# A two-layer convolution block on one core: a third buffer for the residual rows, and small products moved ahead of the big ones

## The chip, the cores and the metric

One core of a Trainium2 chip (trn2) runs the whole program in one launch. The metric is the device time in microseconds of that core, as the median of several runs. Engines are named as the profile names them: PE (matrix products), PEld (loading of the products' fixed operand), DVE (vector), ACT (scalar, with its own DMA queue), POOL (GpSimd) and SP (issues most DMAs and does nothing else).

## The reference

Input x is four images (B = 4) of 64 channels and 256 x 256 pixels, in float32. Two layers follow each other, and each adds its result to its input.

```python
# layer 0: x = x + L0(groupnorm(x)), groups of two channels
h = gelu(conv3x3(x, c1_w) + c1_b)
xa, k = split(c1x1(h, c2_w) + c2_b)            # 64 and 64 channels
xs = gelu(conv_3x1(conv_1x3(xa)))              # one filter per channel
weights = softmax(mean(xs) @ gate_w.T)         # two of three experts are kept
out = xs + sum_i mask_i * c1x1(c1x1(k, w2_i) * c1x1(xs, w1_i), w3_i)   # ranks 2, 4, 8
L0 = c1x1(out, proj_w) + proj_b
# layer 1: x = x + L1(groupnorm(x))
w1, w2 = quantize(w1), quantize(w2)            # 8 bit grid, one scale per tensor
h = relu(batchnorm(conv3x3(x, w1) + b1))       # statistics over all four images
h = batchnorm(conv3x3(h, w2) + b2)
L1 = relu(h + x)
```

The mean over all pixels in the gate of layer 0, and the batch norm of layer 1, make it necessary that a whole image (or all four) has passed one stage before the next begins.

## The kernel before, in words

The two partition halves hold two blocks of rows of the 64 channels. A chunk is 128 partitions by 2048 numbers (1 MB), and an image has 16 of them (`NCH`).

**Layer 0, the slots.** After the statistics of image 0, the program runs 64 slots, one per chunk of the four images, with one slot per chunk `u`. A slot is two steps of a plan: `at_slot(u, pos, ...)` files a call, positions below 6 in the first step and the others in the second. The plan is sorted by step and position and played in that order, and every engine keeps to it. So an instruction that waits holds up all that comes later on its own engine or queue. In a slot PE does:

- at 1 and 1.3 the products (1, 2) and (3, 4) of a 3x3 convolution in a transformed domain (`front_conv`, PSUM tag "c", two buffers, the tile `ps_c`),
- at 2 and 4 the taps of the depthwise filter for an earlier chunk (`front_taps_a`, `front_taps_b`; tile `ps_a`, a single buffer),
- at 5 the products (0, 5), which are added on top of what DVE's `butterfly_c` (4.05) left in the same PSUM tile,
- at 7 and 9 the other half of the taps,
- at 8, between those two, the low-rank branches: `front_k` in even slots (tile `ps_k`), `front_q` in odd ones (tile `ps_q`), both in the single buffer of PSUM tag "p".

The single `ps_a` buffer comes free when ACT (`front_taps_i`, L699) and DVE (`front_taps_h`, L706 to L717) have turned it into the tile `t`. A slot's inner products leave through `front_h(u, True)` on ACT (L658), after DVE's `butterfly_d`; that frees the buffer into which the next slot's products (1, 2) go.

**Layer 0, the outputs.** Once the gate of image b is known, from slot 16(b+1)+4 on, each slot also makes one chunk of outputs of image b: `out_load` (L835) reads the chunk of x into a tile `y` of pool tag "o" with two buffers, `out_open` forms the product, `out_add` (L880, DVE) adds, and `out_store` (L893) writes the tile to `y_d` in DRAM. The statistics of image b+1 or b+2 are read and made in the same slots (`stats_load`, L410; `stats_group` on DVE, `stats_piece` on ACT). The last five chunks of image 2 and all of image 3 are done later, beside layer 1 (`plan_out_late`).

```python
def out_load(b, k):
    ys[b, k] = chunk_out(f"y_{b}_{k}", "o", 2)
    nc.sync.dma_start(flat(ys[b, k]), io["xp"][b, k])
```

**Layer 1.** `plan_conv1` starts in the last slots of layer 0. Each chunk's results h (`conv1_out`, L318 on DVE) are written into a tile and stored to `h1_d`. Odd chunks use `chunk_x`, a place that layer 0 has left, even ones and the first three the single buffer "h1" of the pool `conv1`. After all four images come the second convolution (`conv2`), which keeps to PE, and the end, which reads and writes whole chunks by DMA.

`weights1` makes the quantized weights of layer 1 on DVE during image 0; `stats_end` turns an image's statistics into mean and scale.

Of the kernel before, what the change touches and what calls it, by code (L numbers as in the profile page):

```python
# [9 lines left out]
F32 = mybir.dt.float32  # L10
# [9 lines left out]
P = 128  # L20
# [21 lines left out]
def conv_preact_kernel(ctx: ExitStack, tc: tile.TileContext, io, col128, colset, col64):  # L42
# [81 lines left out]
    nc.vector.memset(eps, GN_EPS)  # L124
    eps_bn = const.tile([P, 1], F32, name="eps_bn")
    nc.vector.memset(eps_bn, BN_EPS)
    zeros = const.tile([P, PW], F32, name="zeros")
# [11 lines left out]
    end, ends, edge_bias = column("end", 2), column("ends", 2), column("edge_bias", 2)  # L139
    outer = lconst.tile([P, 2, W], F32, name="outer")  # L140
    u_raw = lconst.tile([P, 6, 3, C], F32, name="u_raw")
# [32 lines left out]
    def weights():  # L174
# [24 lines left out]
        for i in range(2):  # L199
            o = outer[:, i, :]  # L200
            nc.vector.tensor_scalar(o, zeros[:, 0:W], sh_bias, None, ALU.add)
            nc.vector.tensor_tensor(o[:, 0 : W : W - 1], o[:, 0 : W : W - 1], end, ALU.subtract)
            nc.vector.tensor_scalar(o, o, c128("sv")[:, 2 * i : 2 * i + 1], None, ALU.mult)

# [40 lines left out]
    def weights1(name):  # L245

        scale = w_scale[name]
        w = mset[0][:, colset[name][0] : colset[name][1]]
        nc.vector.tensor_scalar(scale, scale, 1.0 / QMAX, None, ALU.mult)
        inv = stat.tile([P, 1], F32, tag="s3", name=f"inv_{name}")  # L250
        nc.vector.reciprocal(inv, scale)
        yield
        nc.vector.tensor_scalar(w, w, inv, ROUND, ALU.mult, ALU.add)
        nc.vector.tensor_scalar(w, w, ROUND, None, ALU.subtract)
        nc.vector.tensor_scalar(w, w, QMAX, -QMAX, ALU.min, ALU.max)
        yield
        g = w.rearrange("p (k o) -> p k o", k=3)
        first, second = g[:, :, 0:P], g[:, :, P : 2 * P]
        nc.vector.tensor_copy(wq[name][:, 0], first)
        nc.vector.tensor_tensor(wq[name][:, 1], first, second, ALU.add)  # L260
        nc.vector.tensor_scalar(wq[name][:, 2], second, -1.0, None, ALU.mult)
# [439 lines left out]
    def front_taps_h(u, sub):  # L701
# [19 lines left out]
        for at_n, i, row in ((0, 0, 0), (NOCT - 1, 1, 2 * GP - 1)):  # L721
            if n == at_n:
                rows = slice(i * C, i * C + C)
                nc.vector.tensor_tensor(t[rows, row, :], t[rows, row, :], outer[rows, i, :], ALU.subtract)

# [33 lines left out]

    def front_q(b, j):  # L760

        ps = ps_q[b, j] = bank("p", f"ps_q_{b}_{j}").rearrange("p s a b -> p s (a b)")
        for s in range(2):
            for i in range(4):
                x = xss[b, 4 * j + i][:, s]
# [67 lines left out]
    def out_load(b, k):  # L833
        ys[b, k] = chunk_out(f"y_{b}_{k}", "o", 2)
        nc.sync.dma_start(flat(ys[b, k]), io["xp"][b, k])  # L835
# [132 lines left out]
    def conv1_out(b, k, g):  # L968
        if g == 0:
            if k % 2 and (b > 0 or k > 2):  # L970
                h_out[b, k] = flat(chunk_x(f"h1_{b}_{k}"))[:, 0 : CPAIR * W].rearrange("p (a b) -> p a b", b=W)
# [111 lines left out]
    def plan_front():  # L1083
# [4 lines left out]
        for u in range(SLOTS):  # L1088
# [34 lines left out]
            if 0 <= u - 1 <= last:  # L1123
# [30 lines left out]
        for i, name in enumerate(("w1", "w2")):  # L1154
            chain = weights1(name)
            for n in range(3):
                at_slot(7 + 3 * i + n, 7.3, next, chain, None)

    def plan_stats(b):
# [4 lines left out]
        for k in range(NCH):  # L1164
# [13 lines left out]
        places = (e, 8.3), (e + 1, 1.25), (e + 1, 1.36), (e + 2, 1.25), (e + 2, 1.36), (e + 2, 4.45), (e + 2, 8.3), (e + 3, 1.25), (e + 3, 1.36)  # L1178
        chain = stats_end(b)
# [26 lines left out]
    def plan_out_late(b, ns, steps, order, end):  # L1206

        for n, step in zip(ns, steps):
# [22 lines left out]
    def plan_conv1(b):  # L1231
# [4 lines left out]
        for k in range(NCH):  # L1236
# [59 lines left out]
    def bn_affine(mv, gamma, beta, out, name):  # L1296

        ms = stat.tile([P, 2], F32, tag="ms", name=f"ms_{name}")
        for _ in combine(mv, B, c128("avg2"), eps_bn, ms, name):
            pass  # L1300
# [334 lines left out]
```

## Time and profile before

| what | us |
|---|---|
| median of 3 runs | 2964.82 (2963.71 to 2973.92) |
| the profiled execution, its time | 2959.65 |
| the profiled execution, its span on the core | 2957.8 |
| PE busy in the span | 2345.4 (79%) |
| DVE busy | 2448.4 (83%) |
| ACT busy | 2007.1 (68%) |
| POOL busy | 1676.8 (57%) |
| DMA moved, mean | 309 GB/s |

In the profiled execution, layer 0's slots run from about 57 to 1252, the first convolution of layer 1 from about 1270 to 1965, the second to about 2524, and the end to 2958. Shares over the whole span mix these stages, so the stages are read one at a time. A slot begins where PE's products (1, 2) begin, which is where a slot's length is read from.

### The profile page before, as it was taken

To read this page: it belongs to the slowest core of one execution; us is meant where nothing else is said; L and a number is where in the kernel's file an instruction comes from. 1 tells how busy PE (TensorE), PEld (TensorE's weight loads), DVE (VectorE), ACT (ScalarE), POOL (GpSimd) and SP (SyncE) were. 2 spreads that over 40 slices of the span, in tenths; PEclk is the share of its full clock that TensorE was granted. 3 is DMA by queue.
4 is the path that set the end of the run, shared out by engine and by line. 5 is a ranking of instruction groups with operands and counts; after the bars stand their busy time and mean duration, and the time that the engine had idled before them with its cause. 6 is when DMAs were issued, how large, how long until landed. Compare 5 with 4: busy or idle time off the path is not lost.

```text
span 2957.8 us, 52737 instructions
## 1 busy us (share of the span) xinstructions
PE 2345.4 (79%) x21576; PEld 1502.1 (51%) x21576; DVE 2448.4 (83%) x2811; ACT 2007.1 (68%) x2183; POOL 1676.8 (57%) x1252
## 2 busy tenths in 40 slices
PE   2888899999999999979999999989999999000000
PEld 1444445444445555546666667867788888000000
DVE  6688678888888988869999999979999898976664
ACT  4777888787776665567676667978888887432221
POOL 6988888787778888733545546735555555000000
PEclk9999999999999999999999999999999999555555
DMA  8665579999999999859999997747777764999999
GB/s 352 233 239 209 199 269 369 354 351 350 355 349 320 320 319 327 290 203 320 343 367 361 332 360 272 270 176 274 258 267 264 270 219 156 375 412 423 420 424 409
DMA packets 135715, 915.35 MB, mean 309 GB/s; under 512 B 14960, under 2 KB 15728, under 8 KB 40880
## 3 DMA queue, kind: packets, MB, share of 16 engines
q1 hardware_dynamic: 107824, 777.74, 71.1%
q10 hardware_dynamic: 27648, 134.23, 11.3%
q8 instruction: 170, 2.79, 0.4%
q14 instruction: 73, 0.60, 0.1%
HBM read 573.74 MB, written 338.17 MB: 308 GB/s over the span
## 4 chain that ended last, share of the span: by engine, by line
PE 50%; DMA 29%; DVE 13%; ACT 3%; POOL 2%; issue 2%; SPq 0%; ACTq 0%; DVEq 0%; POOLq 0%
PE ps_h L296 18%; PE ps_c L513 9%; DMA y<-in_xp 7%; PE ps_a L513 7%; PE ps_h2m L296 6%; DMA y_end<-y_d 5%; DMA y_d<-y 4%; DMA out<-h 4%; DMA h<-h_d 4%; PE ps_o L513 4%; DMA yn<-y_d 3%; PE ps_hm L296 3%; DVE t L714 2%; DVE t L717 2%; PE ps_k L744 1%
## 5 line engine op out<-in xcount | busy, mean ns | idle before, releaser
L296 PE MATMUL ps_h<-diff,w_q 128*128 128x512 f32 x3072 | 755.2, 400 | 12.4 <-DVE h L318 11.9
L296 PEld LDWEIGHTS ps_h<-diff,w_q 128*128 128x128 f32 x3072 | 577.0, 189 | 190.6 <-issue 20.4
L513 PE MATMUL ps_c<-v,us 64*64 64x256 f32 x9216 | 534.0, 380 | 28.6 <-DVE ps_c L644 25.4
L343 POOL TENSOR_TENSOR d<-yn 128x1024 f32<-128x1024 f32 x128 | 348.9, 2745 | 299.3 <-DMA yn<-y_d 164.8
L513 PEld LDWEIGHTS ps_c<-v,us 64*64 64x64 f32 x9216 | 360.7, 134 | 174.4 <-issue 17.6
L343 POOL TENSOR_TENSOR d<-h 128x1024 f32<-128x1024 f32 x126 | 307.1, 2459 | 206.4 <-DVE diff L351 143.6
L513 PE MATMUL ps_a<-h,av 64*64 64x512 f32 x4080 | 386.5, 492 | 47.3 <-DVE t L717 40.1
L318 DVE SCALAR_TENSOR_TENSOR h<-ps_h,scale_w,m 128x1024 f32<-128x1024 f32 x256 | 323.1, 1279 | 78.7 <-PE ps_h L296 56.3
L561 POOL TENSOR_TENSOR x<-x 128x512 f32<-128x512 f32 x256 | 328.8, 1284 | 12.7
L1497 ACT ACTIVATE h<-h,shift,gn 128x2048 f32<-128x2048 f32 (+1 forms) x65 | 134.3, 2067 | 276.0 <-DVE h L1496 273.8
L513 PEld LDWEIGHTS ps_a<-h,av 64*64 64x64 f32 x4080 | 153.7, 133 | 322.2 <-issue 212.8
L382 ACT ACTIVATE junk<-h,less_h 128x2048 bf16<-128x2048 f32 (+3 forms) x134 | 256.2, 1912 | 13.6 <-DVE h L318 13.5
L1496 DVE SCALAR_TENSOR_TENSOR h<-h,inverse,y_end 128x2048 f32<-128x2048 f32 (+1 forms) x65 | 150.5, 2317 | 122.0 <-DMA y_end<-y_d 122.0
L699 ACT ACTIVATE t<-ps_a,tap_bias,m 128x1016 f32<-128x1016 f32 x128 | 153.3, 1197 | 117.0 <-PE ps_a L513 91.4
L880 DVE SCALAR_TENSOR_TENSOR y<-ps_o,ob,y 128x1024 f32<-128x1024 f32 x128 | 164.0, 1281 | 50.9 <-PE ps_o L513 26.6
L730 ACT ACTIVATE xs<-t 128x1024 f32<-128x1024 f32 x128 | 134.8, 1053 | 103.8 <-DVE t L717 90.2
L353 DVE SCALAR_TENSOR_TENSOR diff<-d,gn,diff 128x1024 fp32r<-128x1024 f32 x128 | 202.0, 1608 | 0.9 <-ACT diff L346 0.5
L296 PE MATMUL ps_h2m<-odd,w_q 128*128 128x512 f32 x768 | 193.5, 401 | 5.9 <-ACT odd L359 3.8
L296 PE MATMUL ps_hm<-odd,w_q 128*128 128x512 f32 x768 | 194.0, 402 | 2.8 <-DVE t L717 1.3
L346 ACT ACTIVATE diff<-d 128x1024 fp32r<-128x1024 f32 x128 | 135.3, 1057 | 81.1 <-POOL d L343 79.5
L553 POOL TENSOR_TENSOR x<-x,x 128x512 f32<-128x512 f32 x128 | 160.5, 1275 | 34.2 <-ACT x L547 34.2
L717 DVE SCALAR_TENSOR_TENSOR t<-ps_a,m,t 128x1020 f32<-128x1020 f32 x128 | 163.9, 1280 | 4.6
(256 smaller groups left out, 4235.2 us busy)
## 6 DMA issues: line engine op xcount, KB each, us to landing
x<-in_xc SPq DMA_DIRECT2D x64, 1280.0 KB
h<-h_d SPq DMA_DIRECT2D x64, 1152.0 KB
yn<-y_d SPq DMA_DIRECT2D x60, 1152.0 KB
xs_in<-in_xp SPq DMA_DIRECT2D x64, 1024.0 KB
xs_d<-xs ACTq DMA_DIRECT2D x128, 512.0 KB
xs_in<-xs_d SPq DMA_DIRECT2D x64, 1024.0 KB
y<-in_xp SPq DMA_DIRECT2D x64, 1024.0 KB
y_d<-y SPq DMA_DIRECT2D x64, 1024.0 KB
```

The lines of the kernel that those rows point to most:

```text
L296: nc.tensor.matmul(ps, wq[w][:, kind, kx, :], t[:, rows, kx : kx + W], start=(j == 0), stop=(j == len(terms) - 1))
L318: nc.vector.scalar_tensor_tensor(h.rearrange("p (e k) w -> p e (k w)", e=2), ps.rearrange("p e k w -> p e (k w)"), w_scale[w], m.unsqueeze ...
L343: engine.tensor_tensor(raw.rearrange("p (g r) w -> p g r w", g=2), *pair, ALU.subtract)
L353: nc.vector.scalar_tensor_tensor(lower, raw, scale, upper.bitcast(F32), ALU.mult, ALU.subtract)
L382: nc.scalar.activation(junk[rows, 0:n], flat(h), AF.Square, bias=less[name][rows], accum_out=total)
L513: last[:] = [nc.tensor.matmul(ps[o, at_out[0] : at_out[1], :], w[i], rhs[i], **flags)]
L553: nc.gpsimd.tensor_tensor(x4[:, j - 1], x_rows(u, j + 2), x4[:, j - 1], ALU.subtract)
L561: nc.gpsimd.tensor_tensor(x[:, r : r + 2], x[:, r + 2 : r + 4], x[:, r : r + 2], ALU.subtract)
L699: nc.scalar.activation(t[:, :, inside], ps[:, :, inside], AF.Identity, bias=tap_bias, scale=sh[:, 1:2])
L717: nc.vector.scalar_tensor_tensor(t[:, :, 0 : W - 1], ps[:, :, 1:W], sh[:, 2:3], t[:, :, 0 : W - 1], ALU.mult, ALU.add)
L880: nc.vector.scalar_tensor_tensor(y, ps.rearrange("p x s w -> p x (s w)"), out_bias[b], y, ALU.add, ALU.add)
L1496: nc.vector.scalar_tensor_tensor(at_h, at_h, inverse[:, b : b + 1], y[:, a:e, :], ALU.mult, ALU.add)
```

## The change

It has these parts:

1. A third place for the outputs' tile `y`: chunks with k % 3 == 2 take a tile "third" in the pool `front`, for images 0 and 1 and the first 11 chunks of image 2. Space for it comes from `outer` (two rows of W numbers become one, half the partitions each) and from `eps_bn`, which had the value of `eps`.
2. In slots before 20 (`alone`), `front_k` and the first three of four units of `front_q` move from position 8 to 4.5, ahead of the products (0, 5). The fourth unit of `front_q` stays at 8.
3. `weights1` is cut into four steps rather than three, in other slots. `stats_group` of image 1 moves behind `butterfly_d` (6.125), and the first step of `stats_end` for image 1 from 8.3 to 6.126.
4. The results of chunk 1 of image 0 in layer 1 go to `chunk_x`. The differences of that chunk are made behind the taps of the last slots.
5. `out_store` in `plan_out_late` goes one step later. In SP's order, image 3's stores of `y` from chunk 7 on now stand behind a load `yn`.

```diff
-    outer = lconst.tile([P, 2, W], F32, name="outer")
+    outer = lconst.tile([P, W], F32, name="outer")
...
         nc.vector.reciprocal(inv, scale)
-        yield
         nc.vector.tensor_scalar(w, w, inv, ROUND, ALU.mult, ALU.add)
+        yield
         nc.vector.tensor_scalar(w, w, ROUND, None, ALU.subtract)
+        yield
         nc.vector.tensor_scalar(w, w, QMAX, -QMAX, ALU.min, ALU.max)
...
-    def front_q(b, j):
-        ps = ps_q[b, j] = bank("p", f"ps_q_{b}_{j}").rearrange("p s a b -> p s (a b)")
+    def front_q(b, j, units=range(4)):
+        if 0 in units:
+            ps_q[b, j] = bank("p", f"ps_q_{b}_{j}").rearrange("p s a b -> p s (a b)")
+        ps = ps_q[b, j]
         for s in range(2):
-            for i in range(4):
+            for i in units:
...
     def out_load(b, k):
-        ys[b, k] = chunk_out(f"y_{b}_{k}", "o", 2)
+        if k % 3 == 2 and (b < B - 2 or b == B - 2 and k < 11):
+            ys[b, k] = front_pool.tile([P, CPAIR, W], F32, tag="third", name=f"y_{b}_{k}")
+        else:
+            ys[b, k] = chunk_out(f"y_{b}_{k}", "o", 2)
...
-            if k % 2 and (b > 0 or k > 2):
+            if k % 2:
                 h_out[b, k] = flat(chunk_x(f"h1_{b}_{k}"))...
...
+            alone = u < NCH + 4
             if u % 2 == 0 and 0 <= j < UNITS // 2:
-                at_slot(u, 8, front_k, *divmod(j, NOCT // 4))
+                at_slot(u, 4.5 if alone else 8, front_k, *divmod(j, NOCT // 4))
             if u % 2 and 0 <= j < UNITS // 2:
-                at_slot(u, 8, front_q, *divmod(j, NOCT // 4))
+                if alone:
+                    at_slot(u, 4.5, front_q, *divmod(j, NOCT // 4), range(3))
+                at_slot(u, 8, front_q, *divmod(j, NOCT // 4), range(3 if alone else 0, 4))
...
-            for n in range(3):
-                at_slot(7 + 3 * i + n, 7.3, next, chain, None)
+            for u in ((5, 6, 7, 8), (9, 10, 11, 14))[i]:
+                at_slot(u, 7.3, next, chain, None)
...
-                at_slot(int(s), 4.1 if s - int(s) < 0.5 else 7.25, stats_group, b, *group)
+                early = 6.125 if int(s) < NCH else 4.1
+                at_slot(int(s), early if s - int(s) < 0.5 else 7.25, stats_group, b, *group)
...
-        places = (e, 8.3), ...
+        places = (e, 6.126 if b == 1 else 8.3), ...
...
             if n % 2:
-                at(step + 1, 13.3, out_store, b, n // 2)
+                at(step + 2, 13.3, out_store, b, n // 2)
...
+            behind = b == 0 and k == 1
-            at(*late(up0, 13.12), conv1_upper, b, k, 0)
-            at(*late(up1, 13.14), conv1_upper, b, k, 1)
+            at(*late(up0, 13.36 if behind else 13.12), conv1_upper, b, k, 0)
+            at(*late(up1, 13.37 if behind else 13.14), conv1_upper, b, k, 1)
-            at(*((t, 1.3) if first else late(low0, 13.22)), conv1_lower, b, k, 0)
+            at(*((t, 1.3) if first else late(low0, 13.45 if behind else 13.22)), conv1_lower, b, k, 0)
```

More of the change, by code (lines that the diff above doesn't have):

```diff
@@ L124, in conv_preact_kernel @@
     nc.vector.memset(eps, GN_EPS)
-    eps_bn = const.tile([P, 1], F32, name="eps_bn")
-    nc.vector.memset(eps_bn, BN_EPS)
+    assert BN_EPS == GN_EPS
     zeros = const.tile([P, PW], F32, name="zeros")
@@ L199, in weights @@
         for i in range(2):
[L200 to L203, printed above, removed]
+            rows = slice(i * C, i * C + C)
+            o = outer[rows]
+            nc.vector.tensor_scalar(o, zeros[rows, 0:W], sh_bias[rows], None, ALU.add)
+            nc.vector.tensor_tensor(o[:, 0 : W : W - 1], o[:, 0 : W : W - 1], end[rows], ALU.subtract)
+            nc.vector.tensor_scalar(o, o, c128("sv")[rows, 2 * i : 2 * i + 1], None, ALU.mult)
         nc.vector.memset(wk, 0.0)
@@ L251, in weights1 @@
         nc.vector.reciprocal(inv, scale)
+        nc.vector.tensor_scalar(w, w, inv, ROUND, ALU.mult, ALU.add)
         yield
-        nc.vector.tensor_scalar(w, w, inv, ROUND, ALU.mult, ALU.add)
         nc.vector.tensor_scalar(w, w, ROUND, None, ALU.subtract)
+        yield
         nc.vector.tensor_scalar(w, w, QMAX, -QMAX, ALU.min, ALU.max)
@@ L723, in front_taps_h @@
                 rows = slice(i * C, i * C + C)
-                nc.vector.tensor_tensor(t[rows, row, :], t[rows, row, :], outer[rows, i, :], ALU.subtract)
+                nc.vector.tensor_tensor(t[rows, row, :], t[rows, row, :], outer[rows], ALU.subtract)
     def front_xs(u, sub):
@@ L1175, in plan_stats @@
                 s = slots[k] + group[2] // 2 * per / 2
-                at_slot(int(s), 4.1 if s - int(s) < 0.5 else 7.25, stats_group, b, *group)
+                early = 6.125 if int(s) < NCH else 4.1
+                at_slot(int(s), early if s - int(s) < 0.5 else 7.25, stats_group, b, *group)
         e = NCH * b - 4
-        places = (e, 8.3), (e + 1, 1.25), (e + 1, 1.36), (e + 2, 1.25), (e + 2, 1.36), (e + 2, 4.45), (e + 2, 8.3), (e + 3, 1.25), (e + 3, 1.36)
+        places = (e, 6.126 if b == 1 else 8.3), (e + 1, 1.25), (e + 1, 1.36), (e + 2, 1.25), (e + 2, 1.36), (e + 2, 4.45), (e + 2, 8.3), (e + 3, 1.25), (e + 3, 1.36)
         chain = stats_end(b)
@@ L1298, in bn_affine @@
         ms = stat.tile([P, 2], F32, tag="ms", name=f"ms_{name}")
-        for _ in combine(mv, B, c128("avg2"), eps_bn, ms, name):
+        for _ in combine(mv, B, c128("avg2"), eps, ms, name):
             pass
```

## The prediction, made before the changed kernel ran

> **What bounds the kernel now.** I read first the busy time by stretches, because shares over the whole span mix unlike stages. I asked for three runs of slots: 23 to 25, 26 to 43 and 45 to 62.
>
> ```profile
> core 0: us, PE busy (x) PEld busy (x) DVE busy (x) ACT busy (x) POOL busy (x), PEclk, DMA share, GB/s
> 455.89:511.92 56.03, 55.89 (x805) 28.75 (x800) 50.34 (x64) 45.55 (x65) 45.94 (x43) 1.00 0.99 375
> 511.92:875.53 363.61, 340.23 (x4764) 173.59 (x4760) 300.76 (x392) 283.49 (x398) 282.31 (x282) 1.00 0.96 352
> 894.14:1233.24 339.10, 338.39 (x4764) 175.47 (x4760) 301.68 (x389) 207.21 (x256) 282.34 (x282) 1.00 0.93 321
> ```
>
> A slot is 56.03/3 = 18.68 us in the first stretch, with PE always busy, 363.61/18 = 20.20 us in the second, with 23.4 us of PE idle, and 339.10/18 = 18.84 us in the third, where no statistics are loaded. So slots 26 to 43 are not PE's. Next, for slots 26 to 43, the waits of PE (total us, times, longest), those of SP's queue, and the chain of work in order of time (start, us).
>
> ```profile
> PE ps_a L513 <- DVE t L717: 16.3, 15, 1.9
> ```
>
> ```profile
> SPq L835 <- DMA y_d<-y: 75.9, 18, 7.7
> ```
>
> ```profile
> 508.50 14.60 DMA y_d<-y
> ...
> 523.18 20.57 DMA y<-in_xp
> ...
> 549.11 14.77 DMA y_d<-y
> ```
>
> Every load of a `y` tile (L835, 18 of 18) waited for the store of the tile two chunks back. A store of 14.60 us, a load of 20.57 us, and DVE's two additions with the taps between them (543.83 to 549.09, 5.3 us) make 40.5 us for two chunks, which is the 20.2 us of a slot. DVE's addition waits for the load, and the taps `t` queue behind it, so PE waits for `t`.
>
> In image 0 I read PE's instructions in order of time, over one slot that began at 164.24, and PE's waits from 100 to 420 (second fence).
>
> ```profile
> 173.41 2.82 PE L513 MATMUL ps_c<-v,us 64*64 64x256 f32 x48 [0.77 <-DVE ps_c L644]
> 176.95 2.38 PE L513 MATMUL ps_a<-h,av 64*64 64x512 f32 x24 [0.72 <-DVE t L717]
> 179.26 1.95 PE L744 MATMUL ps_k<-h,wk 64*32 64x512 f32 x32
> ```
>
> ```profile
> PE ps_a L513 <- DVE t L717: 18.9, 20, 1.9
> PE ps_c L513 <- DVE ps_c L644: 13.9, 18, 1.1
> ```
>
> Products (0, 5) wait for the butterfly, then the taps wait for `t`, and only then comes `ps_k`, which needs neither.
>
> Where layer 1 begins, PE stands still once for long (its waits from 1250 to 1345, the chain, and two stretches with the columns as above):
>
> ```profile
> PE ps_h L296 <- DVE h L318: 8.6, 1, 8.6
> ```
>
> ```profile
> 1318.68 11.37 DMA h_d<-h
> ```
>
> ```profile
> 1319.00:1331.52 12.52, 3.95 (x16) 2.56 (x15) 1.35 (x3) 7.06 (x7) 5.62 (x3) 0.77 1.02 369
> 1331.52:1339.40 7.88, 7.88 (x26) 6.23 (x26) 7.84 (x8) 6.59 (x7) 2.96 (x2) 0.72 1.02 195
> ```
>
> DVE cannot write chunk 2's h until chunk 1's has left the single place "h1". The granted clock falls to 0.77 and 0.72 around it.
>
> **The third place for y.** It adds no instruction. A load then waits for the store three chunks back, which began more than a slot before the load's turn and takes 14.6 us, so the wait at L835 goes. What is late next is the DMA engines. A slot with outputs and statistics moves, from the KB of the issues: x 1280, statistics 1024, xs stored 2 x 512, xs read 1024, y read 1024, y stored 1024, ranks written 256 and read 256. That is 6912 KB or 7.08 MB, and 7.08/20.2 is 350 GB/s, at a DMA share of 0.96. If only the idle 4% is won, 352/0.96 = 367 GB/s, or 19.3 us a slot. The first stretch carried 375 GB/s at 0.99: 18.9 us. PE's floor is 18.63. I take 19.05, between the two, a gain of 18 x 1.15 = 21 us. The Trainium skill speaks against this ("DMA: Bandwidth & Descriptors", "Where 436 GB/s comes from"): HBM transfers are bound near 358 GB/s a core. By that rule a slot needs 7.08/358 = 19.8 us and the gain is 18 x 0.4 = 8 us. This trace moved 375 over three such slots, and 420 GB/s in the end's slices, so I follow the row, and keep 8 as the low end. The high end is PE's floor, 18 x 1.57 = 28. The order on SP's queue is the same in these slots. The load is only issued earlier, so x and xs behind it are no longer held.
>
> **k and q ahead of (0, 5), 18 slots (2 to 19).** A slot is now 17.57 us on average (92.79 to 216.76 has seven in 123.97, so 17.7; two neighbours make 17.38 + 17.76). The moved products (1.95 us, or some 1.4 for three units) cover the 0.77 before (0, 5), and push (0, 5) late enough that `t` is ready: 0.72 to 1.13. These are 1.5 to 1.9 us. Against that, in even slots the wait for the tick after the taps, 0.2 us, is bare. PE alone would come to about 16.1. What is late next: from the end of the taps at 172.6, ACT's `t` (1.2), DVE's `t` (2.85), `butterfly_d` (1.4), and then, in ACT's order, a statistics piece ahead of `h`, end at 180.4, which is 7.8 us that the move does not shorten. The next slot's products (1, 2) need that `h`'s PSUM place. The slot's start to the end of the taps is 8.4 us (164.24 to 172.6), so 8.4 + 7.8 = 16.2 is the floor on this ring, and ACT's `t` for the other half now queues behind both `h`. I put the slot at 16.8 rather than 16.2, as these waits seldom fit exactly: 0.8 x 18 = 14 us, from 5 to 23 (1.3 x 18). POOL needs 15.5 us a slot (twelve at about 1.28), so it does not bind. The skill speaks against the split of q: "TensorEngine Tiling (Array Packing)", "Key Properties", says that a change of tiling mode drains the array. Cutting `ps_q` in two adds two changes in nine slots. In the trace `ps_k` (64*32) between products of 64*64 runs in 1.95 with no idle named before or after it, and by start times `ps_q` begins 2.3 us after the taps' 2.38 began. So I price a change at zero to 0.2 us, at most 9 x 0.4 = 4 us, which the low end holds.
>
> **Weights, statistics, outer.** Of the slots, that from 216.76 lasts 19.11: DVE's three operations on `mset` (1.39, 1.51, 1.54 us) stand ahead of `t`, which then was late by 1.24. Spread, with one of about 1.4 us a slot, this costs nothing while DVE has its 3 us of slack. If that cover is gone, it is 1.5 us in each of some eight slots. I count +1.5 here, and as much from the second weight, from `first`'s statistics behind the butterfly and from POOL's sums ahead of its differences (`ps_m_x` waited 0.82): together 3 us, 0 to 5. `outer` removes nothing on the path (it is before slot 0), nor does `eps_bn`.
>
> **Layer 1's start.** With chunk 1 in `chunk_x`, chunk 2's h needs the store of chunk 0, issued at 1303.9, and `m`, ready at 1319.8. PE would go on at 1322.96, the end of its `ps_hm`, not 1331.52: 8.6 us. The pair of `ps_h` after it took 7.94 where later ones take 5.85, at half clock: 2 more. The taps moved ahead of chunk 1's differences take up to 2.7 of the 3.35 us that PE waits for `t` at 1284.55. But the output product at 1342.4 needs its xs, whose load was issued at 1318.97 and by the bytes ahead of it landed near 1337.5. It comes earlier only by what moves the store of ranks at 1315.56 ahead of it on SP, those 2.7 us. So of 13 us some 7 are kept, 3 to 13. From there PE ran without a gap to 1449, 10.53 us a chunk, so it is not lost.
>
> **The later store.** The trace does not show SP with the load ahead. From 1410 to 1810 SP stood 136.7 us waiting for DVE's y at this store; some loads `yn` behind it come earlier. The store itself may come later by the `yn` load's own wait, and the y load two chunks on later by as much. DVE never waited for a y load there, and the load of 1647.5 was used at 1674.5, with a 14 to 21 us transfer, so 6 us are spare. PE's waits in these 400 us sum to 16. I take 0, from -6 to +4.
>
> **Sum.** 21 + 14 + 3 + 7 + 0 = 45 us against the profiled execution, 2959.65 (span 2957.8 and 1.9 around it), gives 2914.6. The median of the runs lies 5.2 higher, so 2919.8. The second convolution (PE at 100%) and the end (DMA share 1.01) keep their 1000 us.
>
> **Rivals.** (a) As summed, with one part or another short: 0.60. (b) The DMA ceiling holds: y loads no longer wait for stores, but slots stay at 19.8 or longer. 8 + 14 + 3 + 7 = 32, 2933. For it: share 0.96 already. Against it: 375 GB/s before. 0.22. (c) The ring through ACT closes: image 0 wins only 3 and the DMA ceiling holds, 8 + 3 + 4 = 15 or less, 2950 to 2960, which is no change. For it: ACT was 74 to 88% busy in image 0. 0.12. (d) Slower. ACT's `h` of (0, 5), now done later, holds up products (3, 4) of the next slot, and `t` behind it the taps. From my sums `h` ends some 1.5 us into the next slot and (3, 4) start at 2.6, so it decides when ACT is more than 1.1 us later. At 2.4 us later in all 18 slots it costs 1.3 x 18 = 23, and if at the same time the third place only moves the wait to a full DMA ring, the 7 us at layer 1 do not pay it: 2981. For it: two statistics pieces stand ahead of `h` in ACT's order. Against it: 180.4 came 1.2 us before the next slot began at 181.62. 0.06. That the change does not do what it says is no case: a third tile removes that wait by construction.
>
> **The numbers.** (a)'s own range is 2900 to 2932, from the ends 28 + 23 and so on that do not all come together. With (b) and part of (c) the range is 2898 to 2952, leaving out the longest of (c), (d) and more than 67 us of gain. What a measurement of this kernel can tell from no change is 0.5%, 15 us, so faster is below 2950: 0.86. Same 0.09, slower 0.05.
>
> **What would show it.** Right: no wait of L835 for `y_d<-y` in slots 26 to 43, slots near 19.0, DMA share at 0.98 or more; in image 0 the two waits gone, slots near 16.8, and a wait of `ps_c` for ACT's `h` in their place; PE idle under 2 us around layer 1's third chunk, the clock not halved there. Wrong: slots of 26 to 43 at 19.8 with x or xs late in place of y; image 0 at 17.5 with waits for ACT; y loads of image 3 that DVE waits for.

## The result, and the profile after

| what | before | after |
|---|---|---|
| median of 6 runs each, on one chip, us | 2973.6 (2963.71 to 2975.74) | 2943.3 (2938.8 to 2949.07) |
| the profiled execution, its span | 2957.8 | 2937.0 |
| ratio of the times | | 0.9908, 95% interval 0.9888 to 0.9928 |

The change makes the kernel faster by 0.9%, which is 27 us by the mean of the runs (the two medians differ by 30). The forecast was 2920: a sum of 45 us below a kernel before whose median stood at 2964.8 then. The prediction's parts can be followed in the profile by the times at which slots and steps begin. In the table each stage's length is compared between the two profiled executions. "Step n" of layer 1 is the n-th chunk whose `ps_hm` begins.

| stage | before, us | after, difference |
|---|---|---|
| start to slot 2 | 92.5 | -1.2 |
| slots 2 to 18 (image 0 alone) | 308.3 | -11.8 |
| slots 19 to 24 | 111.1 | +0.6 |
| slots 25 to 42 (outputs and statistics) | 363.6 | -0.1 |
| slots 43 to 61 | 357.7 | 0.0 |
| slot 62 to layer 1's step 0 | 38.0 | 0.0 |
| steps 0 to 4 | 68.2 | -14.6 |
| steps 4 to 8 | 42.2 | 0.0 |
| steps 8 to 18 | 115.2 | +4.5 |
| steps 18 to 26 | 86.1 | +5.8 |
| steps 26 to 36 | 113.8 | -1.6 |
| steps 36 to 52 | 163.6 | -5.5 |
| the rest | 1097.5 | +3.2 |

(The prediction numbered the stretch from 511.92 to 875.53 as slots 26 to 43. Counted from slot 0 at 56.97 it is slots 25 to 42.) A stage that a kernel leaves alone came out up to 5 us longer or shorter from one profiled execution to the next, and the last stage up to 8. So a single number of that size is not read, only one that all kernels with a part show and all kernels without it do not.

First the busy time by stretches of after, which answers to the three stretches shown of before. The columns are the window, its length, the busy us of PE, PEld, DVE, ACT and POOL, then the granted clock, the DMA share and GB/s.

```profile
443.04:499.60 56.56, 55.83 (x806) 29.25 (x802) 50.35 (x64) 45.50 (x65) 45.81 (x43) 1.00 1.01 388
499.60:863.10 363.50, 340.59 (x4767) 173.75 (x4762) 300.73 (x392) 283.58 (x397) 282.57 (x282) 1.00 0.96 351
881.70:1220.80 339.10, 338.38 (x4764) 174.73 (x4760) 301.70 (x389) 207.22 (x256) 282.31 (x282) 1.00 0.93 322
```

The middle line is the surprise. A slot still takes 363.50/18 = 20.2 us, PE is still idle for 23 us, and 351 GB/s at a share of 0.96 is what it was (352 at 0.96). Yet the wait that the third place was to remove is gone. These are SP's waits in this stretch (line, waited for, total us, times, longest):

```profile
SPq L899 <- DVE y L886: 90.5, 18, 9.0
SPq L850 <- DMA xs_in<-in_xp: 30.9, 9, 4.2
...
SPq L411 <- DMA y<-in_xp: 21.9, 9, 3.4
SPq L899 <- DMA y_d<-y: 20.2, 7, 3.2
...
SPq L841 <- DMA y<-in_xp: 18.0, 7, 2.9
```

L841 is the load of `y` (L835 before). It waited 75.9 us for stores; now it waits 18.0 for earlier loads, and only once, for 5.9 us, for a store. The rest has moved to other issues, above all to the store of `y` (L899), which waits for DVE's addition. Before, that line was:

```profile
SPq L893 <- DVE y L880: 66.1, 18, 6.8
```

All of SP's waits in these slots sum to 315 us before and 313 us after. The chain of waits shows what stands in the place of the old one (start, length, us):

```profile
508.11 23.03 DMA y<-in_xp
...
531.16 17.53 DMA y<-in_xp
...
548.71 0.34 SPq L411
...
549.10 21.98 DMA y<-in_xp
```

Before, store, load, additions and store made two slots of 40.5 us. Now load follows load, 23.03 and 17.53, which is 40.6 for two slots. What ties one load to the next is a completion semaphore: the DMAs use eight in turn (more of them below), so at 531.16 and at 548.71 SP waited until the load of `y` that had the same one had landed. Two loads take as long as store, load and additions did together. DVE still waits for loads of `y` (11.8 us, 16.1 before), and PE still waits for the `t` that DVE makes:

```profile
PE ps_a L514 <- DVE t L718: 14.6, 14, 1.8
```

In image 0 PE's instructions over one even and one odd slot (start, length, instruction, idle before):

```profile
166.30 0.66 PE L514 MATMUL ps_a<-h,av 64*64 64x256 f32 x8 [0.22 <-DVE tick_v L507]
166.89 1.95 PE L745 MATMUL ps_k<-h,wk 64*32 64x512 f32 x32
168.77 2.82 PE L514 MATMUL ps_c<-v,us 64*64 64x256 f32 x48
```

```profile
182.99 0.66 PE L514 MATMUL ps_a<-h,av 64*64 64x256 f32 x8 [0.53 <-DVE tick_v L507]
183.58 1.92 PE L769 MATMUL ps_q<-xs,m 128*32 128x512 f32 x12
185.43 2.82 PE L514 MATMUL ps_c<-v,us 64*64 64x256 f32 x48
188.07 2.33 PE L514 MATMUL ps_a<-h,av 64*64 64x512 f32 x24
190.33 1.90 PE L769 MATMUL ps_q<-xs,m 128*32 128x512 f32 x4
```

Both waits of before, for the butterfly and for `t`, are gone. What is left of PE's waits between 91.6 and 387.9 is led by the ticks (6.1 and 4.7 us; a tick is a one-column memset, on DVE or POOL, that PE waits for where its products change the PSUM bank), and ACT's `h` costs 0.7 us in all:

```profile
PE ps_a L514 <- DVE tick_v L507: 6.1, 22, 0.6
PE ps_a L514 <- POOL tick L507: 4.7, 6, 1.9
...
PE ps_c L514 <- ACT h L659: 0.7, 2, 0.4
```

But the odd slot runs `ps_q` twice, 1.92 and 1.90, where before it ran once in 1.92.

Slot by slot the gain is uneven. The even slots 2 to 10 are 1.0 to 1.9 us shorter than before, slots 3, 5, 7 and 11 only by 0 to 0.4, slot 9 by 1.4 and slot 12 by 3.4. Slots 13 to 18 have won nothing; together they are 1.2 us longer. In these six POOL is busy for 88% (97.21 of 110.09 us), about as much as before, and now PE waits for it, 8.3 us in all (277.81 to 387.90):

```profile
PE ps_a L514 <- POOL tick L507: 4.7, 6, 1.9
PE ps_c L514 <- POOL x L562: 2.3, 1, 2.3
PE ps_m_x L268 <- POOL x L562: 1.3, 1, 1.3
```

Where layer 1 begins, the wait of 8.6 us for `h` and the low clock around it are gone (granted clock 1.00 from 1284 to 1320). The products follow each other:

```profile
1295.95 1.92 PE L769 MATMUL ps_q<-xs,m 128*32 128x512 f32 x16
1297.81 5.92 PE L297 MATMUL ps_h<-diff,w_q 128*128 128x512 f32 x24
1303.68 3.07 PE L297 MATMUL ps_hm<-odd,w_q 128*128 128x512 f32 x12
1306.59 5.84 PE L297 MATMUL ps_h<-diff,w_q 128*128 128x512 f32 x24
...
1315.39 1.09 PE L514 MATMUL ps_o<-xs_in,m 64*64 64x512 f32 x8
```

### The profile page after: what moved, and what is told of

It reads as the page before. It is cut to its first block, busy times and chain, and to the rows that moved or that the text cites. A ratio compares the mean times of both kernels' runs of the same rounds, so it can differ in the third digit from the quotient of the medians.

```text
span 2937.0 us, 52720 instructions
## 1 busy us (share of the span) xinstructions
PE 2353.1 (80%) x21576; PEld 1498.5 (51%) x21576; DVE 2439.1 (83%) x2810; ACT 2006.9 (68%) x2183; POOL 1680.6 (57%) x1252
## 3 DMA queue, kind: packets, MB, share of 16 engines
q10 hardware_dynamic: 27648, 134.23, 11.5%
## 4 chain that ended last, share of the span: by engine, by line
PE 44%; DMA 35%; DVE 11%; POOL 4%; ACT 3%; issue 2%; SPq 0%; ACTq 0%; DVEq 0%; POOLq 0%
PE ps_h L297 18%; DMA y<-in_xp 14%; PE ps_c L514 8%; PE ps_h2m L297 6%; PE ps_a L514 5%; DMA y_end<-y_d 5%; DMA h<-h_d 4%; DMA out<-h 4%; DMA y_d<-y 3%; PE ps_o L514 3%; DMA yn<-y_d 3%; PE ps_hm L297 2%; DVE diff L354 1%; POOL x L562 1%; PE ps_q L769 1%
## 5 line engine op out<-in xcount | busy, mean ns | idle before, releaser
L514 PE MATMUL ps_c<-v,us 64*64 64x256 f32 x9216 | 535.1, 380 | 16.8 <-DVE ps_c L645 7.8
```

Source lines behind the costliest of these rows:

```text
L514: last[:] = [nc.tensor.matmul(ps[o, at_out[0] : at_out[1], :], w[i], rhs[i], **flags)]
```

## Experiments

All ratios are against the kernel before, run beside it on the same chip. "Profiled" differences are read as in the table above.

### The parts one at a time

The third place alone (part 1):

```diff
+        if k % 3 == 2 and (b < B - 2 or b == B - 2 and k < 11):
+            ys[b, k] = front_pool.tile([P, CPAIR, W], F32, tag="third", name=f"y_{b}_{k}")
+        else:
             ys[b, k] = chunk_out(f"y_{b}_{k}", "o", 2)
```

> The kernel before with the third place for y alone. Theory A (the DMA side limits slots 26 to 43: what was a wait for a store becomes a wait for a load): slots 26 to 43 stay at 20.2 us within 0.2, SP's loads of y wait for no store, the time is that of the kernel before within 5 us. Theory B (the third place won its 20 us and something else in the changed kernel took them back in the same slots): slots near 19.0 and 15 to 25 us less.

Measured: 2965.76 against 2967.44, ratio 0.9988 [0.9969, 1.0008]. Slots 25 to 42 took 20.02 us each in the profile. The third place by itself gives nothing that this measurement can tell from zero.

Parts 2 and 3 alone (k and q earlier, weights and statistics in other places):

```diff
+            alone = u < NCH + 4
-                at_slot(u, 8, front_k, *divmod(j, NOCT // 4))
+                at_slot(u, 4.5 if alone else 8, front_k, *divmod(j, NOCT // 4))
...
+            for u in ((5, 6, 7, 8), (9, 10, 11, 14))[i]:
+                at_slot(u, 7.3, next, chain, None)
...
+                early = 6.125 if int(s) < NCH else 4.1
```

> The kernel before with only image 0's part: k and q ahead of the products (0, 5), the weights and statistics spread. If the parts add up, layer 0's slots 3 to 19 are 11 to 13 us shorter as in the changed kernel and all later stages keep their lengths: 10 to 14 us less. If later stages only take up slack that image 0 gave them, under 5 us less.

Measured: 2952.0, ratio 0.9952 [0.9934, 0.9971]. Slots 2 to 18 are 11.7 us shorter in the profile, which is all of what the whole change wins there.

Part 4 alone (chunk 1's results in the place of x):

```diff
-            if k % 2 and (b > 0 or k > 2):
+            if k % 2:
...
+            behind = b == 0 and k == 1
```

> The kernel before with only chunk 1's results in the place of x and its differences behind the taps. Theory A (given back by DMA): the stretch from the first to the fifth group of odd products of layer 1 is 14 to 15 us shorter, and 6 to 10 of these are lost again over the next hundred microseconds or two, in waits for y loads: 4 to 9 us less in all. Theory B (kept): 13 to 15 us less; then the loss belongs to the later store or to another part.

Measured: 2953.87, ratio 0.9961 [0.994, 0.9982]. Profiled: steps 0 to 4 shorter by 14.8 us, then 4.4 and 5.8 us longer in steps 8 to 18 and 18 to 26. So the time given back belongs to this part, not to the later store or the third place.

The sum of the three is 0.12 + 0.48 + 0.39 = 0.99%, and the whole change measured 0.92%: the parts add up, within intervals of 0.2% each.

The whole change without part 5 (the store of y back at its old step):

```diff
-                at(step + 2, 13.3, out_store, b, n // 2)
+                at(step + 1, 13.3, out_store, b, n // 2)
```

> The changed kernel with image 3's stores of y where they were. Theory A (the later store helps layer 1 from chunk 7 of image 3 on, where the changed kernel won 5.8 us between 1634 and 1802): 3 to 8 us slower than the changed kernel. Theory B (that gain is slack made up after a late start): the same as the changed kernel within 3 us.

Measured: 2942.85, ratio 0.991 [0.9877, 0.9944]. In the time of the whole kernel, with an interval of some 10 us to each side, the later store is worth nothing that can be told from zero. The stage in which it acts says more. Steps 36 to 52 take 164.6 us here and 158.0 in after. The five profiled kernels without the later store take 163.6 to 166.1 there, the nine with it 155.5 to 159.9. With the store at its old step PE waits there for loads of gelu(x), 1.8 to 5.0 us; with the later store for 0 to 1.9 us, in after not at all. In this kernel (1677.62 to 1842.18):

```profile
PE ps_o L514 <- DMA xs_in<-xs_d: 4.4, 2, 3.2
```

So the later store wins some 5 to 6 us in its steps. The spans of this pair of profiles hide them, above all as the last stage, which the store leaves alone, happens to be 7.6 us shorter here.

The whole change without the third place:

```diff
-        if k % 3 == 2 and (b < B - 2 or b == B - 2 and k < 11):
-            ys[b, k] = front_pool.tile([P, CPAIR, W], F32, tag="third", name=f"y_{b}_{k}")
-        else:
-            ys[b, k] = chunk_out(f"y_{b}_{k}", "o", 2)
+        ys[b, k] = chunk_out(f"y_{b}_{k}", "o", 2)
```

> The kernel after with the third place taken out again: y in two places as before, all other parts kept. If the third place is worth nothing also beside the other parts, the ratio is that of the kernel after, 0.991 (within 0.002), and the slots of the stretch 499.6:863.1 stay at 20.2 us. If it is worth in company what it was not worth alone (the other parts bring the stretch on earlier), this kernel is the slower by some 5 us, near 0.993.

Measured: 2944.52, ratio 0.9918 [0.9903, 0.9933], the same as after within the intervals. The profile of this kernel makes the point sharper. Its stretch of slots 25 to 42, and SP's longest wait in it:

```profile
501.16:862.04 360.88, 340.14 (x4764) 173.93 (x4760) 300.35 (x392) 283.68 (x397) 282.73 (x282) 1.00 0.96 354
```

```profile
SPq L838 <- DMA y_d<-y: 73.9, 18, 7.7
```

The wait is back in full, 73.9 us and 18 of 18, and the slots take 20.05 us. Over the profiled executions that left the DMAs of these slots alone, kernels with two places show 20.20, 20.12, 20.03 and 20.05 us a slot, and kernels with three 20.19, 20.02, 19.99, 19.99 and 20.51.

### What sets the 20.2 us of slots 25 to 42

Two DMAs of 512 bytes more in each of slots 24 to 43. Each DMA of this program uses one of eight completion semaphores in turn (in the trace of after, the 975 DMAs share eight, 121 or 122 each), and its issue waits until the DMA that last had it has landed, so at most eight are in flight. Such a wait is `SPq L411 <- DMA y<-in_xp` above: a load of one tile waits for the load of another. A slot issues 8.5 DMAs on average.

```diff
+    def tiny(u, i):
+        t = stat.tile([P, 1], F32, tag="tiny", name=f"tiny_{u}_{i}")
+        nc.sync.dma_start(t, io["m128"][:, 0:1])
...
+            if 24 <= u < 44:
+                at_slot(u, 0.25, tiny, u, 0)
+                at_slot(u, 2.05, tiny, u, 1)
```

> The changed kernel with two more DMAs of 512 bytes each on SP in each of 20 slots (24 to 43); the data goes nowhere. Theory A (bytes: the DMA engines' rate limits these slots): 7.08 MB stay 7.08 MB, the stretch of 18 slots stays at 363.5 us within 4, DMA at about 351 GB/s. Theory B (places in flight: a DMA is issued only when the eighth before it, over SP's and ACT's queues, has landed, so the number of DMAs limits): 10.5 DMAs a slot instead of 8.5, 20.2 x 10.5/8.5 = 25 us, or at least over 21 us a slot.

Measured in a single run: 2966.08. The stretch:

```profile
506.39:888.25 381.86, 346.27 (x4765) 179.86 (x4761) 300.19 (x391) 283.16 (x397) 281.64 (x281) 0.98 0.94 331
```

18.2 us more than before (363.6) for practically no bytes, 21.2 us a slot, and only 331 GB/s. Slots 22 to 24, of which the last has the tiny DMAs too, are 7.0 us longer than in after. So bytes alone, for which 4 us were expected at most, are not the whole of it. A DMA more is not free here. The lower mark that was set for the places, over 21 us a slot, is just met; the 25 us that they alone would make are not. 5.7 of the 18 us are PE's busy time, at a granted clock of 0.98 (346.27 against 340.59 in after), and the other 12.7 are PE's idle time.

The other way round: half of each statistics load of images 2 and 3 left out. Their statistics are made from the first half of each chunk twice, so the results for those images are others. The number of DMAs and all other work stay.

```diff
-        nc.sync.dma_start(flat(x_in[b, k]), io["xp"][b, k])
+        n = CPAIR * W // (2 if b > 1 else 1)
+        nc.sync.dma_start(flat(x_in[b, k])[:, 0:n], io["xp"][b, k][:, 0:n])
```

> The changed kernel with half of each statistics load of images 2 and 3 left out (their statistics are made of the first half of each chunk twice, so the output differs). 0.52 MB less a slot, the same number of DMAs. Theory A (bytes): 6.56 MB at 351 GB/s are 18.7 us, PE's own 18.6: the stretch of 18 slots falls from 363.5 to 336 to 342, and PE's waits for t go. Theory C (order: SP stands at the store of y until DVE has added): the store waits as long as before, the stretch falls by less than half of that, to 350 or more.

Measured in a single run: 2926.23. The stretch:

```profile
500.20:846.01 345.81, 339.49 (x4765) 174.73 (x4761) 302.55 (x392) 283.56 (x398) 282.76 (x282) 1.00 0.95 342
```

Half a MB less a slot takes 17.8 us out: 19.2 us a slot, and PE is busy for 98% of it. So with fewer bytes in as many DMAs these slots shorten until PE binds. A halved load also gives its place among the eight back sooner, so bytes and places are not quite parted by this run.

The store of y issued behind the next slot's load of y, so that SP does not stand at the store (L899, 90.5 us of waits above) with a load behind it:

```diff
-                at_slot(u, 8.25, out_store, b, k)
+                at_slot(*((u, 8.25) if k == NCH - 1 else (u + 1, 2.1)), out_store, b, k)
```

> The changed kernel with each slot's store of y behind the next slot's load of y on SP's queue (the last chunk of an image where it was), which the third place allows. Theory A (bytes): the 90 us that SP stood at that store vanish, the stretch of 18 slots does not move by more than 4 us. Theory C (order): the 4% of idle DMA go, 351 to 366 GB/s, the stretch falls from 363.5 to about 349, 10 to 15 us less in all.

Measured: 2950.16, ratio 0.9939 [0.9914, 0.9963], and the stretch 7.1 us longer than before's, which neither theory expected:

```profile
503.44:874.12 370.68, 345.88 (x4764) 177.55 (x4760) 300.35 (x392) 284.70 (x398) 282.27 (x282) 0.98 0.94 345
```

5.7 of the 7.1 us are PE's busy time (345.88 against 340.23), at a granted clock of 0.98; idle it is hardly longer than before. The wait at the store is nearly gone (1.7 us for DVE's `y`), but SP stands in other places, and the loads of `y` wait for stores again:

```profile
SPq L780 <- DMA ranks<-low_d: 94.8, 8, 13.1
SPq L841 <- DMA y_d<-y: 66.0, 17, 5.4
```

So this order brings nothing. As it undoes what the third place had done, it does not show that no order of SP's could help.

One store of gelu(x) of 1 MB a chunk in place of two of 512 KB on ACT's queue, so 7.5 DMAs a slot with the same bytes:

```diff
     def xs_store(u, sub):
         b, k = divmod(u, NCH)
-        n = 2 * k + sub
-        nc.scalar.dma_start(xs_d[b][:, n, :], flat(xss[b, n]))
+        if sub:
+            at_d = xs_d[b][:, 2 * k : 2 * k + 2, :].rearrange("p a b -> p (a b)")
+            nc.scalar.dma_start(at_d, pairs.pop((b, k)).rearrange("p a b c -> p (a b c)"))
```

> The kernel after, with the two stores of gelu(x) of one chunk (512 KB each, ACT's queue) put into one of 1 MB when its second half is there: the same bytes, 7.5 DMAs a slot instead of 8.5. Two extra DMAs without bytes had made the slots of 499.6:863.1 longer by 18.2 us, half a us for each DMA and slot. If the places among the eight DMAs in flight bind that stretch in their own right, one DMA less a slot gives it back 9 us (and some in the stretch before it, where the same store is made): total near 2930 against 2939 profiled. If bytes bind and the tiny DMAs only cost by waiting in line behind large ones, the stretch keeps its 20.2 us a slot within 4 us and the ratio stays that of the kernel after, 0.991. A third way: the store comes later by half a slot, and the gelu of the next chunk waits for its place; then the slots grow by what ACT waits for tile xs.

Measured: 2946.22, ratio 0.9924 [0.9904, 0.9944].

```profile
506.24:872.23 365.99, 340.98 (x4764) 173.94 (x4760) 301.18 (x392) 284.11 (x397) 282.80 (x282) 1.00 0.93 348
```

One DMA less a slot brought nothing (20.33 us), where two more had cost 1 us a slot. So at 8.5 a place more does not help, while fewer bytes did: taken together the two runs speak for the bytes. Whether the two tiny ones cost time by the place that they hold or by SP's turn is not told apart by these runs. The larger store also goes out later and holds its place for longer, which could hide a small gain.

### q in one piece

The whole change, with `front_q` left whole at its old place; only `front_k` moves.

```diff
-                if alone:
-                    at_slot(u, 4.5, front_q, *divmod(j, NOCT // 4), range(3))
-                at_slot(u, 8, front_q, *divmod(j, NOCT // 4), range(3 if alone else 0, 4))
+                at_slot(u, 8, front_q, *divmod(j, NOCT // 4))
```

> The changed kernel with the q products in one piece at their old place, only k moved. In the trace after, three units of q took 1.92 us and the fourth alone 1.90, as all four together did. Theory A (the four units run side by side, so the cut doubles q's time and odd slots gain nothing): odd slots of image 0 stay near 17.5 us, the time is that of the changed kernel within 3 us. Theory B (the early units do cover the waits): odd slots get longer by 0.7 or more, 6 us or more in all.

Measured: 2943.17, ratio 0.9914 [0.9889, 0.9939]. Slots 2 to 18 are 11.8 us shorter than before, exactly as with the cut. PE in the odd slot that corresponds to the one shown above:

```profile
184.69 2.82 PE L514 MATMUL ps_c<-v,us 64*64 64x256 f32 x48 [0.86 <-DVE ps_c L645]
188.14 2.38 PE L514 MATMUL ps_a<-h,av 64*64 64x512 f32 x24 [0.63 <-DVE t L718]
190.45 1.92 PE L769 MATMUL ps_q<-xs,m 128*32 128x512 f32 x16
```

The two waits, 0.86 and 0.63, are back, and one `ps_q` of 1.92 takes the place of two that take 1.92 and 1.90. The cut of q fills 1.5 us of idle time with 1.9 us of work that wasn't there before.

The start times also show a price of the change of tiling. In after, eight products of `ps_a` are followed once by `ps_q` (182.99, then 183.58, in the odd slot shown above) and once by another 64*64 product:

```profile
158.08 0.66 PE L514 MATMUL ps_a<-h,av 64*64 64x256 f32 x8
158.56 5.37 PE L514 MATMUL ps_c<-v,us 64*64 64x256 f32 x96
```

That is 0.59 us from start to start against 0.48. Over all 67 places in the trace where `ps_q` or `ps_k` follows without a wait, it begins 0.31 us after the last product of `ps_a`; `ps_c` begins 0.20 us after it. So a change of tiling takes some 0.11 us here (the load of the new operand is not told apart from it). A cut of q adds two changes, an estimated 0.2 us.

### Where layer 1's early start is given back

The whole change, with the 21 chunks of x that the late outputs add loaded at half size. The loaded half is added twice, so that part of the outputs is another.

```diff
+        if halved(b, k):
+            first = ys[b, k].rearrange("p a b -> p (a b)").rearrange("p (x u f) -> p u x f", x=2, u=2)[:, 0]
+            n = CPAIR * W // 2
+            nc.sync.dma_start(first, io["xp"][b, k][:, 0:n].rearrange("p (x f) -> p x f", x=2))
```

> The kernel after, where the 21 chunks of x that the late outputs (image 2 from chunk 11, image 3) add come in at half their size: one half of each chunk is loaded and added twice, so that part of the outputs is another. 0.5 MB less a chunk, the same number of DMAs. If what was given back after layer 1's earlier start (4.5 and 5.8 us in the 201 us from its eighth step on) was given back to a full DMA line, the steps from there to the thirty-sixth, 319 us with some 14 of those chunks, shorten: by up to 14 x 1.45 us = 20 us at 361 GB/s, at least by the 10 us given back, until PE alone binds (96% busy late in it). If instead the y_d store and load of a place in turn (latency, two places) or PE's order bind it, the shortening stays within 4 us.

Measured in a single run: 2919.46. Steps 8 to 36, first in after, then in this kernel:

```profile
1354.61:1678.35 323.74, 305.97 (x1489) 207.09 (x1488) 294.95 (x325) 220.17 (x214) 161.10 (x60) 0.98 0.94 351
```

```profile
1355.11:1663.99 308.88, 300.38 (x1490) 204.26 (x1488) 291.16 (x323) 219.80 (x214) 161.59 (x60) 1.00 0.94 341
```

14.9 us shorter: more than the 8.6 that after had given back in these 28 steps (323.74 against before's 315.11). 5.6 of the 14.9 are PE's busy time at a higher granted clock, the rest its idle time. PE's waits for `h` are 1.8 us in before, 9.9 in after and 1.2 here. First before, then after:

```profile
PE ps_h L296 <- DVE h L318: 1.8, 2, 1.2
```

```profile
PE ps_h L297 <- DVE h L319: 9.9, 9, 3.5
```

SP's wait for the store of a y tile stays nearly what it was, 135.1 us in after and 123.0 in this kernel:

```profile
SPq L844 <- DMA y_d<-y: 123.0, 15, 16.3
```

So in part of these steps too the bytes bind, and that wait of the y loads is again not what bounds them. It fits that PE, which starts 14.6 us earlier, runs into transfers that don't come sooner. The half load shows that fewer bytes would free these steps; that the extra 8.6 us of after are made of nothing else is argued from it, not shown.

### The place put to another use

If bytes bind and the wait doesn't, the 1 MB place is worth more as a store that spares transfers. Here it keeps gelu(x) of three chunks in turn from their making to their use, and their stores and loads go away. The outputs are the same.

```diff
+    kept = dict.fromkeys(((0, 0), (1, 4), (2, 8)))
...
+        if (b, k) in kept:
+            if sub == 0:
+                kept[b, k] = front_pool.tile([P, 2, 2, GF], F32, tag="third", name=f"xs_{b}_{k}")
+            x = xss[b, n] = kept[b, k][:, sub]
...
     def xs_store(u, sub):
         b, k = divmod(u, NCH)
+        if (b, k) in kept:
+            return
```

> The kernel after, with the third place used for another thing: y has two places, and the 1 MB place keeps gelu(x) of one chunk on chip from its making to its use 19 slots later, for three chunks in turn (image 0 chunk 0, image 1 chunk 4, image 2 chunk 8), whose two stores of 512 KB and one load of 1 MB go away. The same outputs, 6 MB less moved, 5 MB of them in slots 19 to 61, where the DMA line is full. Bytes theory: 5 MB at 0.35 MB/us, 14 us less than the kernel without the third place, ratio near 0.986. If the order of the y loads and stores bound those slots, or PE in the second half of them, nothing, 0.991.

Measured: 2936.78, ratio 0.9885 [0.9869, 0.9902]; the kernel without the third place, timed beside it, had 0.9918 [0.9903, 0.9933]. By the runs it is the fastest of the kernels that do the whole work, by some 8 to 10 us against the one without; the two intervals just do not overlap. The profiled execution doesn't show it (span 2935.0 against 2934.1). Its lines for slots 25 to 42 and 43 to 61:

```profile
500.19:862.94 362.75, 341.26 (x4764) 174.96 (x4760) 299.94 (x392) 283.79 (x398) 282.93 (x282) 1.00 0.96 348
862.94:1220.74 357.80, 357.02 (x5021) 184.66 (x5016) 316.80 (x408) 222.88 (x277) 297.71 (x296) 1.00 0.92 317
```

In the second stretch PE is busy for 99.8%, so the load spared there (slot 58) is worth nothing. In the first, one load (slot 39) and the stores of one chunk (slot 42) are spared, 2 MB, which by the 351 GB/s of after would be an estimated 6 us. The stretch takes 362.75 us, against 360.88 without the third place, so this profile shows no gain; nor could it well, as the kernels that left these slots' DMAs alone differ by 9 us there. So that it is a little faster rests on the timed runs alone, and where it wins is open.

## Why the prediction was right and where it was wrong

**The direction, and most of the parts, held.** The kernel is faster by 0.92%, and the measured 2943.3 stands 23 us above the forecast. The sum was 45 us; the profiled executions differ by 20.8. Nearly all of that is one term, the 21 us for the third place; for all the others together 24 were forecast.

**The third place: the step that failed.** The prediction gave it 21 us; alone it measured 0.12% [-0.08, 0.31], some 3.6 us with an interval that holds zero, and without it the change is as fast. The mechanism was half right: the wait of the loads for the stores did go, and "what is late next is the DMA engines" was the next bound. The term that was mis-sized is the rate of those engines. The prediction counted on the idle 4% (19.3 us a slot) and then on a faster rate (19.05), because three slots (455.89 to 511.92) had run at 375 GB/s. Neither came: the share stayed at 0.96, and the eighteen slots ran at 352 GB/s before and at 351 after, wait or no wait. The Trainium skill's figure that it set aside, near 358 GB/s a core ("DMA: Bandwidth & Descriptors", "Where 436 GB/s comes from"), would have made an estimated 8 us of it, closer to the nothing that was measured. It is no ceiling for this core, though: the same trace carries 388 GB/s in three slots and 416 in the end (2600 to 2900). Why these slots stay at 351 with a share of 0.96 the runs don't show. The sum 14.6 + 20.57 + 5.3 = 40.5 looked like a cause because it closed exactly. But with the store out of the chain the loads alone filled the same 40.6 us, so how long a store and a load took was set by what else was in line with them.

**k and q ahead of (0, 5).** Predicted 14 us for 18 slots and 3 for the weights and statistics; measured 11.8 in slots 2 to 18. (The 1.2 us before slot 2 are not theirs: the kernels with the third place alone and with part 4 alone have 1.8 and 1.3 there too.) The two waits went as said. Two steps failed. The first is "some 1.4 for three units": three units of `ps_q` take 1.92 us and the fourth alone 1.90, since the units run side by side, so odd slots win next to nothing, and the cut could have been left out. The second is "0.8 x 18". The 17.57 us that it starts from are the mean of two neighbours, but slots 2 to 18 took 18.1 on average. In slots 13 to 18 nothing was won: PE came to wait for POOL there, of which the prediction said that it does not bind. The even slots 4 to 12, at 15.9 to 16.3 us, did better than the 16.8 that it gave them. The rival of a ring through ACT, and the slower one through ACT's `h`, did not come: that wait is 0.7 us in all of image 0. A change of tiling costs 0.11 us, within the "zero to 0.2" that was allowed for it. Weights and statistics were not run apart from k and q, but the slots point to them: slot 9, an odd one that began at 216.76 and took 19.11, is 1.4 us shorter, with the cut of q and without it, and slot 12 wins some 2 us more than slots 8 and 10. Together that is near the 3 that were predicted.

**Layer 1's start.** Predicted 7 kept of 13. All of it came: steps 0 to 4 are 14.6 us shorter, as the loads of xs did not hold the output product at 1315.39 after all. But 8.6 of it went again in steps 8 to 36, so that about 6 are left, and part 4 alone measured 0.39%, some 11.5 us with an interval from 5 to 18. The number came near for a reason that was wrong: "From there PE ran without a gap to 1449, so it is not lost" is the step that failed. The steps after it were in part bound by DMA bytes, at a share of 0.94, as the half loads show, and the prediction had taken PE's work there for all that counted.

**The later store.** Predicted 0, from -6 to +4. The timed runs cannot tell it from zero, but by the stages it won some 5 to 6 us in steps 36 to 52, a little above the upper end. The prediction weighed the loads `yn` and `y` behind the store; what came earlier to some use were the loads of gelu(x), for which PE no longer waits.

**The rivals.** What came is nearest to (b), the DMA ceiling, which had 2933: in it the third place still won 8 us. Had it been put at 0 and the rest left, the sum would have been 24 and the forecast about 2941. That this would have stood so close to 2943 is in part luck: image 0 fell some 5 us short of its 17, and the 5 to 6 of the later store were in no sum.

## What to carry to other kernels

When a load waits for a store and the DMA share is 0.96, ask first what the loads will do once they start earlier: if the slot's bytes over the steady rate of that very stretch already make the slot, a further buffer moves the wait and takes nothing away. Take the rate from the stretch in question, not from a shorter and better one beside it, and test it by halving a transfer before a buffer is built. A batch of small products that run side by side costs its full time for any part of it, so cut it only where the idle time it fills is longer than that. And read a gain per slot in every slot before multiplying it: in six of seventeen slots here another wait took the place of the old ones.

## What the runs showed of the hardware

- Three of the four 128*32 units of `ps_q` take 1.92 us, one alone 1.90, and all four 1.92. They run in parallel, as the Trainium skill ("TensorEngine Tiling (Array Packing)", "Key Properties") says of tiles.
- Between products of 64*64 and of 128*32 or 64*32 a change of tiling takes some 0.11 us by start times (0.31 us from the last product to the next, where 0.20 without a change).
- Two DMAs of 512 bytes more in a slot that issued 8.5 cost 1.0 us a slot (18.2 over 18 slots, 5.7 of them PE's busy time at a granted clock of 0.98); one DMA less, with the same bytes, saved nothing.
- The DMA share doesn't say how many bytes a second go with it: 351 GB/s at 0.96 in slots 25 to 42, 388 at 1.01 in the three slots before, 331 at 0.94 with the tiny DMAs.
